# Routing tables and sums of a fused two-layer kernel in free columns of a PSUM bank

## The chip, the cores and the metric

The kernel runs on one core of one Trainium2 chip. A core has five engines that run their own instruction queues side by side: PE (TensorE, matrix products into PSUM), DVE (VectorE), ACT (ScalarE), POOL (GpSimd) and SP (SyncE, which starts transfers). SBUF is the working memory of all of them; PSUM, in eight banks of 2 KB a partition, is written by PE and read and written by VectorE and ScalarE. The metric is the device time of one execution in microseconds (us), as the median of several runs.

## What is computed

Four layers with residuals over x of 8 batches, 512 steps and 128 channels, all in float32: a bounded linear recurrence, one linear layer picked out of eight, a delta rule with 16 heads of 8 channels, and a mixture of 8 experts of which each token takes 2. The two that matter here, cut to the core:

```python
# the delta rule: S is 8 x 8 for each batch and head, 512 steps one after the other
def step(S, inp):
    q_t, k_t, v_t, beta_t = inp
    retrieval = jnp.einsum('bhij,bhj->bhi', S, k_t)
    S = S + jnp.einsum('bhi,bhj->bhij', beta_t * (v_t - retrieval), k_t)
    o_t = jnp.einsum('bhij,bhj->bhi', S, q_t)
    return (S, o_t)

# the experts: of 8, each token takes the 2 with the largest probability
logits = xf @ w_router
probs = jax.nn.softmax(logits, axis=-1)
topk_w, topk_idx = jax.lax.top_k(probs, TOP_K)
mask = jax.nn.one_hot(topk_idx, NUM_EXPERTS, dtype=xf.dtype)
weights = jnp.sum(topk_w[..., None] * mask, axis=1)
h = jax.nn.gelu(jnp.einsum('te,ieh->tih', xf, w1) + b1)
out = jnp.einsum('tih,ihe->tie', h, w2) + b2
out = jnp.sum(out * weights[..., None], axis=1)
```

## The kernel before

**Tiles and stages.** A tile is 128 tokens: 16 steps of 8 batches. The 32 tiles pass in nine pieces of 2, 4, 4, 4, 4, 4, 4, 4 and 2 tiles (SIZES) through the layers. For each piece `scanned`, `ssm_out` and `linear` do the first two layers, `delta_in` prepares keys, queries and the small triangular matrices of the delta rule (`tmat`, made by GpSimd), `delta_rule` runs the recurrence, `route` picks the experts. Pieces are gathered into groups (GROUPS) of one or two; when a group is complete, `experts` sorts its tokens by expert and runs them. The last piece has no sorting; `every_expert` runs all experts on it.

**The recurrence.** It goes in 128 blocks of 4 steps. Each block is six VectorE instructions, each of which needs the one before (lines 1404 to 1423): a sum of the 8 retrieval products of the block before (`st<-so`, 320 elements a partition), the product with the triangular matrix (`prod<-tmat,st`, 128), its sum (`st<-prod`), the product with the keys (`st<-kq,st`, 256), the sum onto the state (`st<-st`, 320) and the product of the state with keys and queries (`so<-kq,st`, 512). The state and all small sums of the recurrence live in two PSUM banks, `st0` and `st1`, in turn from block to block. Of their 512 columns, 320 hold the terms of the state (NS) and 32 the retrieval sums; the block's right-hand sides `u_16` take 128 more in `st1`. In `st0` the last 160 columns are not used. After each tile ScalarE copies `u_16` out (`upd<-st`).

**The routing.** `route` takes the two best experts of each token with VectorE's max and max_index (`best`, `besti`) and compares the indices with a table of 0 to 7, `iota8i`, to get one-hot masks (`mine`, once for each of the nine pieces). GpSimd then counts and weighs them. `experts` (five times, for the groups that are sorted) turns the counts into places: PE sums them over the tokens into a PSUM bank (`totals`, `earlier`), and VectorE makes from that, in thirteen small instructions and two more ahead of them (`mask`, `runf`): `full` (which blocks of 128 an expert fills, against a table `thresholds` of multiples of 128), `nblks`, `ends` and `starts` (blocks of each expert and their running sum), `place` (twice added to, then shifted by `starts`), `chosen` and `destf` (each token's two places), `dest` (the same as integers), `of_block` and `expert` (which expert a block belongs to, against a table `iotab` of 0 to 23), and `where` (twice: the rows at which that expert's weights start). GpSimd scatters the rows to `places` by `dest`; SP loads blocks of rows (`xb`) and an expert's first weights (`w1b`) by `where`; PE and ScalarE do the two layers (`ph`, `hid`, `po`), and GpSimd gathers the results (`back`).

**What sets the order.** A planner (`Plan`) records every operation and can lay them out by costs and due times. Here it does not: ORDER (line 383) lists all 4796 operations by number in a fixed order, and BANKS the PSUM bank of each product in turn; `ordered` (line 189) takes both as they are, so each engine's queue is this order. Routing instructions stand in VectorE's queue between those of the recurrence. What an instruction waits for is written by the framework below the planner, from what the instruction reads and writes; `region` and `depend` (lines 84 and 96) only serve the planner's own search for an order. A helper at line 330 issues nearly all operations, so most rows of the profile carry that line.

**Where the tables are.** `iota8i` and `iotab` are made at lines 866 to 883 with GpSimd's iota, `thresholds` at line 885 (tile at 884) by VectorE from `iotab`; `nblks`, `destf`, `expert` and `place` are tiles of SBUF (`gtile`). All of the routing's small instructions thus read SBUF alone, but for `runf` and the two sums of `place` (`totals` and `earlier` are in PSUM).

Of the kernel before, what the change touches and what calls it, by code (L numbers as in the profile page):

```python
# [16 lines left out]
P = 128  # L17
# [52 lines left out]
class Plan:  # L70
# [12 lines left out]
    @staticmethod  # L83
    def region(x):
        if isinstance(x, Bank):
            return x.owner, None, 0, 1, 0, 1
        name, dims, at = x.tensor.name, x.ap, x.offset
        if x.space == bass.MemoryType.DRAM:
            return name, None, 0, 1, at, at + sum((n - 1) * s for s, n in dims) + 1
        row = dims[0][0]  # L90
        p, f = divmod(at, row)
        if x.space == bass.MemoryType.PSUM:
            return name, None, 0, 1, 0, 1
        return name, None, p, p + dims[0][1], f, f + sum((n - 1) * s for s, n in dims[1:]) + 1
# [259 lines left out]
def _cost(engine, name, n, kw):  # L354
# [284 lines left out]
def seq_kernel(  # L639
# [215 lines left out]
    for base_, step in ((0, 1), (DH - 1, -1)):  # L855
# [7 lines left out]
            channel_multiplier=step,  # L863
        )

    iota8i = ctile([P, NE], "iota8i", U32)
    nc.gpsimd.iota(iota8i, pattern=[[1, NE]], base=0, channel_multiplier=0)

    before_ones = ctile([P, P], "before_ones")
# [24 lines left out]

    st = [bank(f"st{i}") for i in range(2)]
    NS = DH * B * (BL + 1)

    def terms(n):  # L900
# [1120 lines left out]
```

## Time and profile before

| what | us |
|---|---|
| median of 3 runs | 665.15 |
| lowest and highest of them | 662.67, 671.21 |
| the profiled execution's own time | 665.96 |
| its span, first to last instruction | 664.3 |
| PE busy | 526.6 (79%) |
| VectorE busy, 1290 instructions | 465.0 (70%) |
| ScalarE busy | 468.5 (71%) |
| GpSimd busy, 603 instructions | 458.8 (69%) |
| mean granted clock of PE | 0.915 |
| bytes moved by DMA | 110.16 MB, 166 GB/s |

The page divides the span into 40 slices of 16.6 us and gives each engine's busy share in tenths. Its chain of work that ended last follows back from the last instruction, at each step to what released it or to the instruction before it on its engine: VectorE holds 34% of the span, PE 26%, ScalarE 15%, GpSimd 12%. A group's row names line, engine, operation and tiles (written <- read), the shape and the count, then busy time, mean duration, and the idle time before it with what ended it. A row in order of time has the start, the duration, the engine and the same names. A duration counts from an instruction's start to its end, so what it waits for after its start is in it.

### The profile page before, as it was taken

The page shows a single profiled execution, that of the slowest core. Times are in us where ns is not written, and L with a number is a line of the kernel's source. Part 1 is how long each engine was busy: PE and PEld are TensorE (multiplying, and loading weights), DVE is VectorE, ACT ScalarE, POOL GpSimd, SP SyncE. Part 2 cuts the span into 40 slices and gives each one's busy share as a digit, 9 for nine tenths or more (in the row PEclk, how much of TensorE's full clock was granted, in tenths as well). Part 3 has the DMA queues.
Part 4 walks back from the last instruction along what each step waited for, and adds up shares of the span by engine and source line. Part 5 has one row for each costly group of instructions (what it writes and reads, how often), then busy time and mean ns, then how long its engine had stood idle before and what let it go on. Part 6 is the DMA issues. An engine that isn't in the chain of part 4 may idle for free.

```text
span 664.3 us, 10937 instructions
## 1 busy us (share of the span) xinstructions
PE 526.6 (79%) x3077; PEld 409.9 (62%) x3077; DVE 465.0 (70%) x1290; ACT 468.5 (71%) x984; POOL 458.8 (69%) x603
## 2 busy tenths in 40 slices
PE   3885668687796688796888787989969888879876
PEld 3653234454554465674676575787958887768775
DVE  6667158999988999989899998998991770002021
ACT  2875887879768579988899997857855654636421
POOL 6545567768768748899986978885588678454340
PEclk9899778989679789989899898999989999898988
DMA  4948145235243557446875576788877876766631
GB/s 127 318 136 273 56 117 144 64 84 154 64 127 74 160 144 189 132 128 171 213 193 152 145 193 176 208 233 224 220 227 199 236 226 216 203 207 191 169 103 35
DMA packets 96722, 110.16 MB, mean 166 GB/s; under 512 B 10180, under 2 KB 68207, under 8 KB 96663
## 3 DMA queue, kind: packets, MB, share of 16 engines
q1 hardware_dynamic: 91984, 101.31, 54.6%
q0 software_dynamic: 3904, 8.00, 4.3%
q8 instruction: 26, 0.43, 0.3%
q14 instruction: 34, 0.27, 0.1%
q10 hardware_dynamic: 774, 0.15, 0.1%
HBM read 85.90 MB, written 27.48 MB: 171 GB/s over the span
## 4 chain that ended last, share of the span: by engine, by line
DVE 34%; PE 26%; ACT 15%; POOL 12%; issue 6%; DMA 3%; another core or an unknown queue 2%; ACTq 1%; SPq 1%; DVEq 0%; POOLq 0%
DVE st L330 16%; PE in L330 9%; PE ph L330 8%; DVE so L330 6%; POOL places L1685 4%; PE po L1747 4%; ACT f L330 3%; PE po L330 3%; DVE prod L330 3%; ACT hid L330 2%; ACT L299 2%; ACT b L330 2%; POOL so L330 2%; PE in L1747 2%
## 5 line engine op out<-in xcount | busy, mean ns | idle before, releaser
L330 PE MATMUL ph<-xbT,w1b 128*128 128x128 f32 x760 | 141.1, 287 | 12.3 <-ACT xbT L330 5.5
L330 PEld LDWEIGHTS ph<-xbT,w1b 128*128 128x128 f32 x760 | 113.9, 199 | 19.6 <-ACT xbT L330 7.7
L330 ACT ACTIVATE hid<-ph 128x512 f32<-128x512 f32 x111 | 65.5, 598 | 78.4 <-PE ph L330 44.7
L1747 PE MATMUL po<-w_sb,hid 128*128 x536 | 104.4, 286 | 4.8 <-ACT hid L330 2.9
L1747 PEld LDWEIGHTS po<-w_sb,hid 128*128 128x128 f32 x536 | 84.0, 199 | 15.0 <-issue 9.4
L330 DVE TENSOR_TENSOR so<-kq,st 128x512 f32<-128x512 f32 x128 | 87.6, 684 | 5.6 <-PE in L330 0.6
L299 ACT ACT_TABLE_LOAD x64 | 82.1, 1283 | 8.9 <-DMA hid<-in_L_attn_ln_b_dram 7.8
L1685 POOL DMA_INDIRECT places<-xne,small_dest x60 | 60.0, 1000 | 19.6 <-issue 10.6
L330 POOL DMA_INDIRECT back<-results,small_dest x60 | 58.7, 978 | 21.1 <-issue 14.0
L330 DVE TENSOR_REDUCE st<-st 128x64 f32<-128x320 f32 x128 | 63.6, 497 | 3.7
L330 DVE TENSOR_REDUCE st<-so 128x32 f32<-128x320 f32 x128 | 62.8, 491 | 3.9 <-ACT so L330 0.8
L330 DVE TENSOR_TENSOR st<-kq,st 128x256 f32<-128x256 f32 x128 | 54.5, 426 | 3.5
L330 PEld LDWEIGHTS po<-wo,so 128*128 128x128 f32 x240 | 40.2, 213 | 23.4 <-POOL so L330 9.1
L330 PE MATMUL po<-wo,so 128*128 128x128 f32 x240 | 48.1, 303 | 8.3 <-POOL so L330 6.1
L330 PE MATMUL in<-b,wqkvb 128*128 128x512 f32 (+1 forms) x72 | 39.2, 635 | 11.5 <-ACT b L330 3.6
L1747 PE MATMUL in<-w_sb,hid 128*128 x224 | 45.6, 288 | 1.4 <-DVE small_where L330 1.0
L330 PE MATMUL in<-f,wT 128*128 128x512 f32 (+1 forms) x72 | 39.8, 646 | 8.3 <-DVE small_best L330 3.7
L330 DVE TENSOR_REDUCE st<-prod 128x32 f32<-128x128 f32 x128 | 37.2, 291 | 6.2 <-ACT upd L330 1.6
L330 DVE TENSOR_TENSOR prod<-tmat,st 128x128 f32<-128x128 f32 x128 | 36.3, 284 | 7.4 <-POOL tmat L330 4.2
L330 POOL TENSOR_TENSOR f<-f,f 128x512 f32<-128x512 f32 (+1 forms) x27 | 32.4, 1199 | 12.4 <-ACT f L330 12.3
L330 POOL TENSOR_TENSOR so<-so 128x512 f32<-128x512 f32 x24 | 31.3, 1304 | 11.4 <-DVE so L330 8.5
L330 POOL TENSOR_TENSOR fin<-fin,back 128x512 f32<-128x512 f32 (+1 forms) x14 | 16.8, 1198 | 29.9 <-ACT back L330 29.7
(339 smaller groups left out, 1380.3 us busy)
## 6 DMA issues: line engine op xcount, KB each, us to landing
kq<-scratch SPq DMA_DIRECT2D x64, 512.0 KB
w1b<-w1b_dram SPq DMA_DIRECT2D x103, 256.0 KB
xb<-places SPq DMA_DIRECT2D x20, 256.0 KB
results<-yb SPq DMA_DIRECT2D x20, 256.0 KB
places<-yb SPq DMA_DIRECT2D x2, 1472.0 KB
kq<-in_L_ffn_w_dram SPq DMA_DIRECT2D x2, 1024.0 KB
w1b_dram<-kq SPq DMA_DIRECT2D x2, 1024.0 KB
u_rows<-in_L_attn_u_dram SPq DMA_DIRECT2D x7, 256.0 KB
```

Source lines behind the costliest of these rows:

```text
L299: self.hw.scalar.preload_act_table_set(switch)
L330: return method(*(on(x) for x in args), **{k: on(x) for k, x in kw.items()})
L1685: rows_out = hw.gpsimd.indirect_dma_start(out=table[0 : nblk * P, :], out_offset=bass.IndirectOffsetOnAxis(ap=at, axis=0), in_=src, in_off ...
L1747: return hw.tensor.matmul(out_.on(nc.banks), lhsT=src, rhs=w2_f[:, bass.ds(at + c * P, P)], start=(c == 0), stop=(c == NHB - 1),)
```

## The change

Four of the routing's small sums and the two tables they are compared with move from SBUF to the 160 unused columns of `st0`: `iotab` (24 columns), `thresholds` (8), `nblks` (8), the last value of `place` (64), `destf` (16) and `expert` (23), 143 in all. `iota8i` and its iota on GpSimd are dropped: `mine` compares with the first eight columns of `iotab` instead, a float32 operand beside the uint32 indices. The first of the two sums of `place` stays in SBUF, the second writes PSUM. The clearing of `st0` at the start leaves the last 160 columns out. `region` keeps the columns of `st0` and `st1` apart for the planner. ORDER is the same with the number of the dropped iota taken out and those after it lowered by one; BANKS is unchanged.

```diff
-        if x.space == bass.MemoryType.PSUM:
+        if x.space == bass.MemoryType.PSUM and not name.startswith("st"):
             return name, None, 0, 1, 0, 1
...
-    iota8i = ctile([P, NE], "iota8i", U32)
-    nc.gpsimd.iota(iota8i, pattern=[[1, NE]], base=0, channel_multiplier=0)
...
-    iotab = ctile([P, MAXB + 1], "iotab")
+    st = [bank(f"st{i}") for i in range(2)]
+    NS = DH * B * (BL + 1)
+    spare = st[0][:, NS + B * BL :]
+    taken_of_spare = [0]
+
+    def spared(*shape):
+        n = math.prod(shape)
+        at = taken_of_spare[0]
+        taken_of_spare[0] = at + n
+        assert at + n <= N - NS - B * BL
+        return view(spare[:, at : at + n], [P, *shape])
+
+    iotab = spared(MAXB + 1)
     nc.vector.tensor_copy(iotab, iotabi)
-    thresholds = ctile([P, MAXT], "thresholds")
+    thresholds = spared(MAXT)
+    nblks_of, place_of, destf_of, expert_of = spared(NE), spared(NE * MAXT), spared(2, MAXT), spared(MAXB)
     nc.vector.tensor_scalar_mul(thresholds, iotab[:, 0:MAXT], float(P))
...
-    nc.vector.memset(st[0], 0.0)
+    nc.vector.memset(st[0][:, 0 : NS + B * BL], 0.0)
     nc.vector.memset(st[1], 0.0)
...
         nc.vector.tensor_tensor(
             mine,
-            iota8i.unsqueeze(1).unsqueeze(1).to_broadcast([P, 2, NT, NE]),
+            iotab[:, 0:NE].unsqueeze(1).unsqueeze(1).to_broadcast([P, 2, NT, NE]),
...
-        nblks = gtile([P, NE], "nblks")
+        nblks = nblks_of
...
-        nc.vector.tensor_add(place, place, earlier)
+        nc.vector.tensor_add(place_of[:, 0 : NE * nt], place, earlier)
+        place = place_of[:, 0 : NE * nt]
...
-        destf = gtile([P, 2, MAXT], "destf")[:, :, 0:nt]
+        destf = destf_of[:, :, 0:nt]
...
-        expert = gtile([1, MAXB], "expert")[:, 0:nblk]
+        expert = expert_of[0:1, 0:nblk]
```

More of the change, by code (lines that the diff above doesn't have):

```diff
@@ L893, in seq_kernel @@
     nc.vector.tensor_copy(iotap, iotapi)
-    st = [bank(f"st{i}") for i in range(2)]
-    NS = DH * B * (BL + 1)
     def terms(n):
```

490 rows, old and new, of the table ORDER are left out of this document.

## Prediction

> **What bounds the kernel now.** I read the page's engine rows and slices first, then the groups of VectorE by form, then single instructions in order of time, then the chain of waits. The slices say where VectorE can matter: it is 80 to 100% busy from the seventh slice (100 us) to the thirtieth (498 us), and idle for long stretches after that, where PE works through the experts.
>
> ```profile
> PE   3885668687796688796888787989969888879876
> DVE  6667158999988999989899998998991770002021
> POOL 6545567768768748899986978885588678454340
> ```
>
> The groups of VectorE show what the change is about: the same size of instruction takes two kinds of time.
>
> ```profile
> L330 DVE TENSOR_REDUCE st<-st 128x64 f32<-128x320 f32 x128 | 63.6, 497 | 3.7
> L330 DVE TENSOR_REDUCE st<-so 128x32 f32<-128x320 f32 x128 | 62.8, 491 | 3.9 <-ACT so L330 0.8
> L330 DVE TENSOR_TENSOR prod<-tmat,st 128x128 f32<-128x128 f32 x128 | 36.3, 284 | 7.4 <-POOL tmat L330 4.2
> L330 DVE TENSOR_TENSOR x<-po,base 128x128 f32<-128x128 f32 x15 | 4.3, 285 | 29.3 <-remote 20.0 <-PE po L330 9.3
> L330 DVE TENSOR_TENSOR small_mine<-iota8i,small_besti 128x64 f32<-128x64 uint32 x7 | 3.9, 564 | 0.0
> L330 DVE TENSOR_TENSOR small_starts<-small_ends,small_nblks 128x8 f32<-128x8 f32 x5 | 3.1, 614 | 0.0
> L330 DVE TENSOR_TENSOR small_chosen<-small_chosen,small_place 128x128 f32<-128x128 f32 x3 | 2.8, 930 | 0.0
> ```
>
> Products with one operand in PSUM (prod from st, x from po) average 284 and 285 ns for 128 elements, and in the per-tile view they never leave 256 to 295 ns in 143 executions, whatever GpSimd did. With both operands in SBUF, 8 elements (small_starts) average 614 ns and 128 (small_chosen) 930. The order of time shows why.
>
> ```profile
> 216.14 2.35 POOL L330 TENSOR_TENSOR both<-both,f 128x1024 f32<-128x1024 f32 x1
> 216.53 1.99 DVE L330 TENSOR_TENSOR small_starts<-small_ends,small_nblks 128x8 f32<-128x8 f32 x1
> 218.44 0.68 DVE L330 TENSOR_TENSOR so<-kq,st 128x512 f32<-128x512 f32 x1
> ```
>
> The instruction of 8 elements ends some 25 ns after the GpSimd instruction it ran into. The chain of waits has it in full:
>
> ```profile
> 215.68 0.53 DVE small_ends L330
> 216.22 0.10 DVE st L330
> 216.31 0.22 issue
> 216.53 1.99 DVE small_starts L330
> 218.51 0.60 DVE so L330
> ```
>
> **What is gained.** I went through each instruction the change touches and took its time less that of an unblocked one. Where a GpSimd instruction stood in front: mine 991, 1544 and 541 against 216 (2.43 us); starts 1985 and 620 against 159 (2.29); ends 623 and 608 against 160, and one of 221 (0.97); chosen 520, 1056 and 1215 against 285 (1.94); full 666, 479 and 290 against 165, 175 and 216 (0.88); place 731 against 203 (0.53); of_block 682 against 329 (0.35); where 1245 and five of 208 to 361 against 155 (1.7). Sum 11.1 us of VectorE. The thresholds at 2.5 us took 2081 ns against 152 for a small one out of PSUM (logs from ph), 1.9 us more.
>
> Only what the chain holds moves the end. At 212 to 219 us it runs through full, ends and starts: 0.50 + 0.46 + 1.83 = 2.8. At 229 us it goes through the GpSimd sum of so that mine (991 ns) stands behind, so prod comes 0.7 earlier. At 274 to 282 it holds of_block, starts, chosen and one where: 0.35 + 0.46 + 0.24 + 0.2 = 1.25. At 392.6 it waits 0.85 us behind chosen: 0.77. Sum 5.5 us. Off the chain lie the mine of 1544 ns at 332.8 (the chain is on GpSimd from 327 to 336.5), that at 371.6 (ScalarE and PE), ends and place at 388 to 390 (ScalarE), chosen at 474.3 (ScalarE's table load, 474.0 to 475.3) and full and where after 541 (PE, ScalarE). The thresholds and the removed iota (125 ns of GpSimd at 8.4 us) are covered by the loads that the chain waits for until 11.1 us: nothing. mask, a copy within SBUF that also waited (657 ns), stays.
>
> **What is paid.** Nine mine and thirteen instructions in each of five routings, 74, get an operand or result in PSUM; 54 read PSUM where they read SBUF alone. From rows: a reduce of 320 elements takes 497 ns out of PSUM and 491 out of SBUF, so 54 x 6 ns = 0.3 us. Results: st from prod, 295 ns, against destf, 268, both reducing 128 elements: 27 ns for 20 results, 0.5 us. A third of both is on the chain, 0.3. [...]
>
> The larger price is a wait. The tables share the bank st0 with the recurrence's state, and this trace shows waits kept by bank, not by columns:
>
> ```profile
> 484.85 0.29 DVE L330 TENSOR_REDUCE st<-prod 128x32 f32<-128x128 f32 x1
> 485.18 0.43 DVE L330 TENSOR_TENSOR st<-kq,st 128x256 f32<-128x256 f32 x1
> 485.64 0.50 DVE L330 TENSOR_REDUCE st<-st 128x64 f32<-128x320 f32 x1
> 486.17 0.27 ACT L330 COPY upd<-st 128x128 f32<-128x128 f32 x1 [4.13 <-DVE st L330]
> ```
>
> ScalarE's upd copies columns that st from prod finished at 485.14, yet it starts 30 ns after the reduce that merely uses the same bank. Only VectorE touches st0, so no other engine gets a wait, but on VectorE neighbours now overlap and would stop doing so:
>
> ```profile
> 387.84 0.21 DVE L330 TENSOR_TENSOR small_place<-small_runf,in 128x64 f32<-128x64 f32 x1
> 387.97 0.21 DVE L330 TENSOR_REDUCE small_nblks<-small_full 128x8 f32<-128x64 f32 x1
> 388.10 0.21 DVE L330 TENSOR_TENSOR small_place<-small_place,in 128x64 f32<-128x64 f32 x1
> ```
>
> They start 0.13 apart and last 0.21. Counting in VectorE's order every pair of neighbours that overlaps, has one of the 74 in it, and would have one of the two writing st0, I find 44, each losing 0.05 to 0.11 us: 4.4 us. On the stretches of the chain named above (and 472 to 478) that is 2.7 us. Whether an engine gets such waits on itself the trace can't show: bounds 0 and 2.7 on the chain. I take 2.7, as the copies on ScalarE are kept by bank every time. Behind a waiting routing instruction stands the recurrence's next, and behind that the sums of so on GpSimd and PE; this is why I count the wait in full.
>
> Net on the chain: 5.5 - 0.3 - 2.7 = 2.5 us. The profiled execution took 665.96 (span 664.3 plus 1.7 around it), so 663.5; it lay 0.8 above the median of 665.15, so **662.6 us** in the median. Late next are the scatters on GpSimd (283 to 334 us) and PE with its weight loads after 500; GpSimd is 70% busy from 236 to 270, so it can start earlier.
>
> **Rivals.**
> - Hidden by what follows. From 283 to 334 us the chain is GpSimd's, after 490 PE's and the DMAs'. Against it: the scatters wait for dest, which VectorE writes. Time: 665 less half a us, 664.5.
> - Slower: the waits by bank cost more than the lock. It happens where a routing instruction and the recurrence around it line up so that none overlaps. If GpSimd's stretch swallows what is gained before it, 4.4 of waits and 0.8 of PSUM on top of the median less the 0.77 and 0.7 kept gives 668.9. It decides from 5.2 us on the chain. At most, two lost overlaps of 0.1 us for each of 74 are 14.8 us: 680. [...]
> - All of it gained: the off-chain waits were about to be the chain. 11.1 us: 654.1. With the thresholds' 1.9 and the 2.5 us by which GpSimd's slowed instructions (those over 120 ns above the shortest of their form) exceed that shortest, 15.5: 649.7.
> - The change doesn't do it: an instruction with one SBUF operand still waits. Against: 143 executions at 256 to 295 ns. Time 665 to 668.
>
> **How the numbers follow.** Chances: the forecast 0.47, its own range 659.9 (no waits by bank) to 665; hidden 0.15; slower 0.18, half of it over 2%; all gained 0.15, two thirds over 2%; no effect 0.05. Two per cent, 13.3 us, is about what a measurement of this kernel can tell from no change; its runs lie 8.5 us apart (662.67 to 671.21). So faster by over 2% 0.10, slower 0.09, within 0.81. The range goes from 654.1 less the 2.5 us of the lowest run, 652, to 668.9 plus half of the highest run's 6.1, 672; 0.19 is left out.
>
> **What would show it.** In the changed profile mine, starts and ends lie near 216, 160 and 175 ns at most; the chain at 212 to 219 us is 2.8 us shorter. If the waits by bank are there, neighbours like those at 387.8 start 0.23 apart instead of 0.13. The recurrence's last product, at 544.3 us now, comes 2 to 6 us earlier. It is wrong if small instructions with a table in PSUM still last as long as GpSimd's beside them, if the recurrence ends later than now, or if it ends earlier and the span doesn't follow.

## The result and the profile after

| what | before | after |
|---|---|---|
| median of 22 runs each, us | 667.1 | 663.06 |
| lowest and highest, us | 662.67, 671.21 | 658.68, 665.26 |
| the profiled execution's span, us | 664.3 | 661.3 |
| VectorE busy in it, us | 465.0 | 458.0 |
| mean granted clock of PE | 0.915 | 0.909 |

The ratio of the times is 0.9938, 95% interval 0.992 to 0.9956: faster by 4.1 us (2.9 to 5.3), well below the 2% that count as a difference. The change was measured twice more, as x8 and x10 below, 0.9952 (0.9915 to 0.9989) and 0.993 (0.9897 to 0.9962); weighted by their intervals the three give 0.9939 (0.9924 to 0.9953). Every ratio in this document is taken from the fast runs alone and is not the ratio of the two medians beside it, which lies up to 0.003 away (x3: 0.9975 for a ratio of 0.9945; x8: 0.9974 for 0.9952).

VectorE's busy tenths in the page of the changed kernel, 40 slices of 16.5 us:

```profile
DVE  7667158999988999889799998998991760002021
```

The shape is that of before: a VectorE near its limit from 100 to 490 us. Some groups of VectorE's instructions, forms apart (busy us, mean ns of one | idle before):

```profile
L330 DVE TENSOR_TENSOR prod<-tmat,st 128x128 f32<-128x128 f32 x128 | 36.4, 285 | 7.4 <-POOL tmat L330 4.2
L330 DVE TENSOR_TENSOR small_mine<-st,small_besti 128x64 f32<-128x64 f32 x7 | 1.6, 222 | 0.1
L330 DVE TENSOR_TENSOR small_chosen<-small_chosen,st 128x128 f32<-128x128 f32 x3 | 0.9, 289 | 0.3
L330 DVE TENSOR_TENSOR small_starts<-small_ends,st 128x8 f32<-128x8 f32 x5 | 0.8, 154 | 0.0
L330 DVE COPY small_mask<-follows 128x32 f32<-128x32 f32 x1 | 0.7, 668 | 0.0
```

The recurrence's own `prod` costs what it did (285 ns, 284 before). mine fell from a mean of 564 ns to 222, starts from 614 to 154, chosen from 930 to 289: the waits that stood in these durations are gone. Added up over the trace, the 74 instructions that the change touches took 26.2 us before and 15.6 after. mask, which the change leaves in SBUF, still takes 668 ns. The chain of waits at the place where starts had held it for 1.99 us (start, us, what):

```profile
215.60 0.17 DVE small_ends L330
215.77 0.10 DVE st L330
215.87 0.21 issue
216.08 0.15 DVE small_starts L330
216.24 0.66 DVE so L330
```

From the end of `ends` to `so` the chain now spends 0.47 us, of which `starts` has 0.15. The new waits are there as well: at the place that answers to 387.8 us of before,

```profile
386.63 0.21 DVE L330 TENSOR_TENSOR small_place<-small_runf,in 128x64 f32<-128x64 f32 x1
386.76 0.22 DVE L330 TENSOR_REDUCE st<-small_full 128x8 f32<-128x64 f32 x1
387.01 0.23 DVE L330 TENSOR_TENSOR st<-small_place,in 128x64 f32<-128x64 f32 x1
387.28 0.17 DVE L330 TENSOR_TENSOR_SCAN small_ends<-ones,st 128x8 f32<-128x8 f32 x1
```

the first two, of which only one writes `st0`, still start 0.13 us apart; the next two pairs, where both use it, 0.25 and 0.27.

**The ledger by blocks.** One block of the recurrence goes from one `so` product to the next. The length of most blocks hardly depends on how early the block starts (the one at 206.38 us is 2.90 us long, and 2.90 again where it starts at 206.55 in the first profile of the changed kernel and at 203.25 in x8), so two traces can be compared block by block. Of the blocks whose length changed, those at the moved instructions came out as follows (start and length before; difference in the changed kernel, in the first profile and in the two of the later runs x8 and x10):

```
 start  length  after     x8    x10   routing instructions in it
177.55   3.13   +0.10  +0.10  +0.11   mine
209.28   4.00   -0.37  -0.81  -0.45   runf, mask, full
213.28   5.16   -2.03  -2.03  -2.03   place, place, nblks, ends, starts
218.44   2.99   +0.35  +0.35  +0.36   of_block, place, chosen, destf, dest, expert, where
228.28   3.78   -0.58  -0.58  -0.58   mine
270.21   2.96   +1.25  +0.26  +0.26   full, place, place
273.17   4.31   -0.29  -0.29  -0.29   nblks, ends, of_block, starts, place, chosen, destf
277.48   4.03   +0.06  +0.07  +0.07   dest, expert, where
284.71   3.04   -0.15  -0.15  -0.15   where
332.20   4.22   -1.32  -1.33  -1.33   mine
336.42   3.11   +0.29  +0.30  +0.29   (the block behind it)
370.47   3.22   -0.19  -0.20  -0.20   mine
386.53   4.66   -0.58  -0.57  -0.57   full, place, nblks, place, ends, starts, place
391.18   4.43   -0.05  -0.05  -0.05   of_block, chosen, destf, dest, expert, where
469.65   3.48   +0.40  +0.39  +0.41   full, place, nblks, place, ends, starts
473.13   4.30   -0.11  -0.11  -0.10   place, chosen, destf, dest, of_block, expert
534.14   3.49   +0.12  +0.12  +0.12   mine
```

But for the block at 209 us, where mask itself took 0.22 us in x8, and one cell at 270, they agree within 0.02 us. With 0.37 shorter at 209 and 0.26 longer at 270 they sum to 4.1 us shorter. Two blocks with moved instructions are left out, as they differ from execution to execution: the one at 465.9 us, with another mine (+0.18, +0.12, -0.25), and the last, at 537.6, with the fifth routing (-0.16, -0.39, -1.57). Blocks without routing are left out as well, and not all of them are neutral. In the one at 318 us VectorE waits for PE's product `po`, 1.31 us before and 2.07, 1.52 and 2.25 in the three profiles of the changed kernel, and the block became 0.76, 0.21 and 0.94 us longer. So the 4.1 us are a gain in the blocks of routing, not yet one at the end.

### The profile page after: what moved, and what is told of

Its sections match the earlier page's. It is cut to its first block, busy times and chain, and to the rows that moved or that the text cites. A ratio compares the mean times of both kernels' runs of the same rounds, so it can differ in the third digit from the quotient of the medians.

```text
span 661.3 us, 10932 instructions
## 1 busy us (share of the span) xinstructions
PE 527.5 (80%) x3077; PEld 410.6 (62%) x3077; DVE 458.0 (69%) x1290; ACT 469.1 (71%) x984; POOL 458.5 (69%) x602
## 4 chain that ended last, share of the span: by engine, by line
DVE 33%; PE 30%; ACT 15%; POOL 10%; issue 6%; DMA 3%; another core or an unknown queue 2%; SPq 1%; ACTq 1%; DVEq 0%; POOLq 0%
DVE st L330 16%; PE in L330 11%; PE ph L330 9%; DVE so L330 6%; PE po L330 4%; POOL places L1695 4%; PE po L1757 4%; ACT f L330 4%; ACT L299 3%; DVE prod L330 3%; ACT hid L330 2%; PE in L1757 2%; ACT b L330 2%; POOL f L330 1%
## 5 line engine op out<-in xcount | busy, mean ns | idle before, releaser
L1757 PE MATMUL po<-w_sb,hid 128*128 x536 | 105.8, 289 | 3.1 <-issue 2.4
L1757 PEld LDWEIGHTS in<-w_sb,hid 128*128 128x128 f32 x224 | 34.7, 195 | 5.6 <-issue 5.0
```

What stands on the lines that cost most here:

```text
L1757: return hw.tensor.matmul(out_.on(nc.banks), lhsT=src, rhs=w2_f[:, bass.ds(at + c * P, P)], start=(c == 0), stop=(c == NHB - 1),)
```

## The experiments

The first four stand against the kernel before on one chip (its median there 665.89 in 29 runs).

**x1: the waits without the tables.** The kernel before; VectorE's instructions that would share `st0` wait for each other as if they did, all tables and sums stay in SBUF.

```diff
+                if op.st0:
+                    table, reads, writes = op.st0
+                    behind = last.get((not table, True)) if not writes else max(
+                        (last[k] for k in ((not table, True), (not table, False)) if k in last), default=None
+                    )
+                    if behind:
+                        wait = mybir.DependencyInfo(mybir.DependencyClass.Sync, mybir.DependencyReason.DATA)
+                        self.tc.add_manual_dep(made.ins, behind[1], wait, reason="as if in one bank")
```

> The kernel before, its tables in SBUF, with the waits alone that the shared bank brings: each routing instruction waits for the recurrence's neighbour that would touch st0, and the other way round. Theory (the waits by bank are the price of the change): 1.0 to 2.7 us slower than the kernel before, ratio 1.0015 to 1.004, less than the 2.7 counted where a routing instruction stands behind GpSimd anyway; in the trace full, place and nblks start 0.23 to 0.25 us apart where they started 0.13 apart, and starts, mine and chosen still last 0.5 to 2 us. Rival (a wait on the engine's own predecessor costs nothing): ratio 1.000 with its interval on both sides of it.

Measured: 668.73 us, ratio 1.0033 (1.0002 to 1.0064), 2.2 us slower (0.1 to 4.3). Seven blocks with routing in them are longer by 0.14 to 1.02 us, 2.6 in all; left out are the one at 270, where VectorE stood idle for PE, the one at 332, where mine took 0.76 us beside one GpSimd instruction instead of 1.54 beside two and the block was 0.79 shorter, and three with a mine that are 0.1 to 0.2 us longer. So the waits cost time here: in the block at 273, `nblks`, the sum of `so` and `ends` start 0.25 and 0.53 us apart in x1, as in the changed kernel, where they started 0.13 and 0.39 apart before. Their size in time is known only to lie between 0.1 and 4.3 us, and not all of the 2.6 us is spacing: in that block `ends`, started later, took 0.52 us instead of 0.22, up to the end of a GpSimd instruction. The spacing of full, place and nblks that was expected is not there (0.13 us as before): x1's waits are only those between routing and recurrence, and between two routing instructions, such as 386.76 and 387.01 above, it adds none.

**x2 and x3: the halves of the change.** x2 moves the table that mine compares with, nothing else. x3 moves everything else and leaves mine with its table in SBUF.

```diff
+    iota8 = st[0][:, NS + B * BL : NS + B * BL + NE]
+    nc.vector.tensor_copy(iota8, iotabi[:, 0:NE])
...
-            iota8i.unsqueeze(1).unsqueeze(1).to_broadcast([P, 2, NT, NE]),
+            iota8.unsqueeze(1).unsqueeze(1).to_broadcast([P, 2, NT, NE]),
```

> Only the nine mine read a table in PSUM (0 to 7, in st0); all tables and sums of the sorting stay in SBUF. Theory (what counts is the waiting on the chain): the mine of 991 ns was on the chain, those of 1544 and 541 ns were not, so 0.7 us faster than before, ratio 0.999, at most 0.997. Rival (every wait of VectorE counts): 2.4 us of 11, ratio 0.9964, and more than a third of the change's 4.1 us. In the trace all nine mine under 230 ns, starts, ends and chosen as long as before.

> The change without mine: thresholds, iotab and the four sums in st0, mine compares with iota8i in SBUF as before. Theory: the chain at 212 to 219 us and at 274 to 282 us held 2.8 and 1.25 us of these and 0.77 at 392, so most of the change's 4.1 us is here: 2.5 to 3.7 us faster than before, ratio 0.9945 to 0.9962. Rival (every wait counts): the same 2.5 or so that are left after mine's, ratio 0.9975 to 0.996. In the trace three mine of 0.3 to 1.3 us beyond 216 ns, all of the sorting's instructions short.

Measured: x2 666.59 us, ratio 0.9994 (0.9966 to 1.0023); x3 664.25 us, 0.9945 (0.9912 to 0.9978). In x2 all nine mine are short:

```profile
L330 DVE TENSOR_TENSOR small_mine<-st,small_besti x9: 190/211/225, 180.3 to 604.7; 128x64 f32<-128x64 f32 x7, 128x32 f32<-128x32 f32 x2
```

and the blocks of mine change as in the whole change (-0.58 at 228, -1.34 and then +0.30 at 332, -0.21 at 370). The other blocks with routing keep their length within 0.02 us, but for the one at 386, longer by 0.33. What x2 leaves in SBUF need not take the same time twice: mask, which the changed kernel leaves there too, took 0.67 us in its first profile and 0.22 in x8. Which instruction it is at 386 was not shown. In x3 the blocks of the sums change as in the whole change (-2.03 at 213, -0.29 at 273, -0.58 at 386), and those of mine at 228 and 370 do not (0.00 and -0.01). By the ratios most of the time comes from the sums, though the two intervals overlap between 0.9966 and 0.9978. Whether mine adds to it, the interval of x2 (2.3 us faster to 1.5 slower) leaves open. In x2's trace the recurrence's last product comes at 544.5 us, no earlier than before: blocks without mine (0.49 us longer at 318, 0.41 at 382, 0.73 at 528, with waits for PE and for a transfer) took back what those with mine had gained.

**x4: the same step backwards.** The kernel before with the recurrence's retrieval sums `w`, one operand of each `prod`, taken out of PSUM; its other operand, `tmat`, is in SBUF. The sum that writes `w` from `so` then reads and writes SBUF alone as well.

```diff
+    sums = [ctile([P, B * BL], f"w{i}") for i in range(2)]
...
-        return st[n % 2][:, NS : NS + B * BL].rearrange("p (b t) -> p b t", t=BL)
+        return sums[n % 2].rearrange("p (b t) -> p b t", t=BL)
```

> The kernel before with one thing moved the other way: the recurrence's retrieval sums w lie in SBUF and not in st0 and st1, so that each of the 128 products prod reads both operands from SBUF. Theory (two SBUF operands stand behind a GpSimd instruction that is under way): the 39 instructions of that kind in the routing waited 9.4 us, 0.24 each; 128 of them on the recurrence's chain are 31 us at that rate, and what slack the recurrence has takes some: 10 to 31 us slower, ratio 1.015 to 1.047, with prod from 284 ns at the mean to 400 and more and single ones over 1 us. Rival (PSUM isn't what frees them; the routing's instructions were slow for their small size or their place): prod stays within 256 to 300 ns, ratio 1.000.

Measured: 706.97 us, ratio 1.062 (1.0554 to 1.0687), 41 us slower. The rows of the tile `w`, shortest, middle and longest duration in ns:

```profile
L330 DVE TENSOR_REDUCE w<-so x128: 457/485/489, 90.5 to 584.2; 128x32 f32<-128x320 f32 x128
L330 DVE TENSOR_TENSOR prod<-tmat,w x128: 260/293/5698, 94.3 to 585.3; 128x128 f32<-128x128 f32 x128
```

Half of the 128 products are as fast as ever and the mean goes from 284 to 655 ns, so 47.6 us more of VectorE: with its second operand in SBUF the same form took anything from 260 to 5698 ns. The longest, 5.70 us from 458.21, ends 0.16 us after a row of GpSimd instructions without a gap that runs from 457.67 to 463.75; that GpSimd's work of the moment sets the length is read from ends like this one. The sums `w<-so`, with one operand and the result in SBUF, stayed within 457 to 489 ns in 128 executions. So reading and writing SBUF alone did not make every instruction wait; `prod`, with a second operand there, waited. The price was above the range expected.

The next three, x5 to x7, ask whether what the change left can be had, and what becomes of its gain at 270 us (the kernel before on this chip: 667.71, 17 runs). In the first profile of the changed kernel VectorE stood idle there until PE's sums were done:

```profile
270.41 0.29 DVE L330 TENSOR_TENSOR_SCAN small_runf<-follows,in 128x64 f32<-128x64 f32 x1 [0.85 <-PE in L330]
```

**x5: base and mask on ScalarE.**

```diff
-        normalised(x2, rstd, shift, tiles_of(base), 0, g == 0)
+        normalised(x2, rstd, shift, tiles_of(base), 0)
...
-            nc.vector.tensor_copy(mask.rearrange("p (e i) -> p e i", e=NE), follows[:, :, 0:nt])
+            (nc.scalar.copy if nt == 4 else nc.vector.tensor_copy)(mask.rearrange("p (e i) -> p e i", e=NE), follows[:, :, 0:nt])
```

> The changed kernel, with two instructions that still read SBUF alone and still last long beside GpSimd moved to ScalarE: base of the first piece (two of 1.29 us at 60.5 us, 2.51 together) and the mask of the second group (0.67 us at 211.1 us). Theory (what a table in PSUM cannot reach still waits for GpSimd, and the wait counts where VectorE holds the chain): base ends near 61.6 instead of 63.06, the scan z starts 0.9 earlier (GpSimd's decay then sets it), and the recurrence comes 0.3 to 0.5 us earlier still behind 211. If it is carried to the end, 0.8 to 1.4 us off the changed kernel: ratio to the kernel before 0.992 (0.990 to 0.994). Rival (the first 95 us end on loads and PE, and what is gained at 211 is given back behind 270): as the changed kernel, 0.9938; in the trace z earlier, but the recurrence's first product not.

**x6: two instructions exchanged** in ORDER: 2466 (ScalarE's `f`) behind 2172 (its copy out of the bank), 1687 (`earlier`) right behind 1686 (`totals`).

> The changed kernel with two instructions of the order exchanged around 268 us: ScalarE's f_7<-f_7 (0.72 us) goes behind its copy f<-in, which empties the bank that the totals' product needs, and PE's earlier stands right behind totals. Theory (the 0.85 us for which VectorE's runf stands idle at 270.4 us in the changed kernel is the gain handed back to ScalarE and PE, by that bank): the idle time is gone (under 0.2 us), and the recurrence lies some 2 us ahead of the kernel before at 282 us, where the changed kernel lay 1.28 ahead; by the end 0 to 0.8 us of it is left, as at 322 us the chain is on PE and ScalarE: ratio 0.9925 to 0.994. Rival (the hand-over at 270 is not set by that bank but by GpSimd's b and so beside it): idle 0.6 to 0.9 as now, recurrence 1.3 ahead, ratio 0.9938.

**x7: both.**

> Both edits together on the changed kernel. Theory: their gains add up to 270 us (recurrence 2.5 to 3.5 us ahead of the kernel before at 282), and 1 to 2 us of the sum is left at the end: ratio 0.991 (0.989 to 0.9935). Rival (GpSimd, PE and ScalarE between 283 and 334 us take it all back): 0.9938, as the changed kernel.

Measured: 659.16, 660.21 and 661.38 us; ratios 0.9876 (0.9835 to 0.9917), 0.989 (0.9848 to 0.9933) and 0.9886 (0.9856 to 0.9916). In x5 the recurrence's first `so` comes at 99.3 us, 98.6 in the first profile of the changed kernel: nothing is gained at the start, as the rival had it. In x6 the idle time at 270 is gone and the block there is 0.26 longer than before instead of 1.25; but in x5, where nothing was exchanged, it is 0.26 as well. That three kernels with different edits all lie some 0.005 below the first ratio of the changed kernel made the chip a suspect, so the changed kernel was run beside them.

**x8 and x9: the changed kernel and x7 on one chip** (kernel before: 666.12, 17 runs).

> The changed kernel once more, unaltered, so that it and the next run share a chip and the runs of the kernel before. Theory (the change gives 3 to 5 us, by what it measured): ratio 0.992 to 0.9956. In its trace the recurrence lies 2.2 to 2.6 us ahead of the kernel before at 232 to 267 us, as in its first profile; whether VectorE stands idle 0.85 us at 270 us again shows if that hand-over belongs to the order (it comes again) or to one execution (it does not). Rival: the first ratio was one chip's, here 0.996 or more.

> The kernel with both edits once more (base and mask on ScalarE, the two instructions exchanged at 268 us), beside the changed kernel on the same chip. Theory (waits behind GpSimd that the change left, and the hand-over at 270 us, are on the path to the end): 2 to 4 us below the changed kernel, ratio to the kernel before 0.986 to 0.991. Rival (what the edits gain ahead of 540 us is lost after it, where PE and its weight loads set the end, as in the profiled execution of the first run): as the changed kernel, 0.992 to 0.996.

Measured: x8 664.36 us, ratio 0.9952 (0.9915 to 0.9989); x9 660.3 us, 0.9908 (0.9875 to 0.9942). x8 settles the hand-over: unaltered, the changed kernel has no idle time there in this execution, its block is +0.26, and from 209 to 232 us the recurrence gains 3.1 us on the kernel before, 2.66 in the first profile and the rest from mask. The 0.85 us at 270 are in one of the three profiles of the changed kernel. In x8 the recurrence lay 6.2 us ahead at 232 us, not the 2.2 to 2.6 expected, for another reason, told below. x9, 4.1 us below x8 in the median, came out as its theory had it; the next three do not repeat it.

**x10 to x12: the changed kernel, x5 and x7 on one chip** (kernel before: 648.99, 29 runs).

> The changed kernel once more, as the measure for the next two on the same chip. Theory (a gain of some 4 us, by the blocks of the recurrence that hold a moved instruction, which come out alike to 0.05 us in three executions: 4.1 us shorter in all): ratio 0.991 to 0.996. Rival (the ratios of the changed kernel differ by chip as much as by kernel): outside of that.

> The changed kernel with base of the first piece and the mask of the second group on ScalarE. Theory (what is shown of it in the recurrence is one block at 209 us, shorter by 0.82 instead of 0.38 us): 0.4 us below the changed kernel, which is not to be told from it: ratios within 0.002. Rival (the start of the program is on the path to the end, and 0.9 to 1.9 us are gained there as well): 1.5 to 3 us below, a ratio lower by 0.002 to 0.0045.

> That, and the two instructions exchanged at 268 us. Theory (the hand-over at 270 us was one execution's): as the run before, within 0.002. Rival (it recurs in most executions): 0.5 to 1 us lower than the run before.

Measured: 642.95, 644.31 and 644.52 us; ratios 0.993 (0.9897 to 0.9962), 0.9946 (0.9916 to 0.9975) and 0.9925 (0.9895 to 0.9955). Neither edit is to be told from the changed kernel. Moving mask is seen in its block (0.82 shorter instead of 0.45 at 209 us) and nowhere in the time; no version here is shown to beat the changed kernel. The idle time at 270 us is not in x10 either.

## Why the prediction was right, and where it was not

**The gain.** Right in kind: the durations of mine, starts, ends and chosen fell to those of their forms, and x4 shows the reverse with a loss ten times the gain. By place, what was said to be gained on the chain against what the blocks show, the new waits included: 209 to 221 us, 2.8 against 2.05; 229, 0.7 against 0.58; 270 to 285, 1.25 against 0.11; 386 to 395, 0.77 against 0.62. Where the old wait was one long instruction (starts, 1.99 us), nearly all of it came through; where it was three or four short ones, the new waits ate it. In the kernel before, the block at 273:

```profile
273.77 0.21 DVE L330 TENSOR_REDUCE small_nblks<-small_full 128x8 f32<-128x64 f32 x1
273.90 0.48 DVE L330 TENSOR_REDUCE st<-so 128x32 f32<-128x320 f32 x1
274.29 0.22 DVE L330 TENSOR_TENSOR_SCAN small_ends<-ones,small_nblks 128x8 f32<-128x8 f32 x1
...
275.24 0.62 DVE L330 TENSOR_TENSOR small_starts<-small_ends,small_nblks 128x8 f32<-128x8 f32 x1
275.79 0.27 DVE L330 TENSOR_REDUCE st<-prod 128x32 f32<-128x128 f32 x1
```

and in x8, the changed kernel again:

```profile
267.91 0.23 DVE L330 TENSOR_REDUCE st<-small_full 128x8 f32<-128x64 f32 x1
268.18 0.49 DVE L330 TENSOR_REDUCE st<-so 128x32 f32<-128x320 f32 x1
268.70 0.17 DVE L330 TENSOR_TENSOR_SCAN small_ends<-ones,st 128x8 f32<-128x8 f32 x1
...
269.24 0.14 DVE L330 TENSOR_TENSOR small_starts<-small_ends,st 128x8 f32<-128x8 f32 x1
269.31 0.27 DVE L330 TENSOR_REDUCE st<-prod 128x32 f32<-128x128 f32 x1
```

From `ends` to the sum of `prod` 1.50 us became 0.61, as forecast; but `nblks`, the sum of `so` and `ends`, which had started 0.13 and 0.39 us apart, now start 0.27 and 0.52 apart, and the block ahead of it and the one behind lose 0.26 and 0.07 in the same way.

**The price.** Right in kind and somewhat high. That VectorE gets waits on itself by bank, which the trace of before could not show, is shown by the spacing above: the instructions at 386.76, 387.01 and 387.28 each use other columns of `st0` than the one ahead, and start 0.25 and 0.27 us apart where it was 0.13 before. x1 writes such waits between routing and recurrence, with the same spacing (0.25), and puts their price between 0.1 and 4.3 us. On the four places 5.5 us of gain left 3.36, so 2.1 were paid if the 5.5 came in full; with the 0.29 net at 469 to 478 it is 2.4, where 2.7 of waits and 0.3 of PSUM were taken. In the changed kernel they are seen alone where no old wait was: +0.35, +0.26 and +0.40 in the blocks at 218, 270 and 469. The cost of an operand in PSUM is as small as taken: `nblks` went from 0.21 to 0.23 us at 273, `st` from `small_chosen`, which was destf, from 0.27 to 0.29.

**The step that failed.** "Off the chain lie the mine of 1544 ns at 332.8 (the chain is on GpSimd from 327 to 336.5), that at 371.6 (ScalarE and PE)". The block at 332 became 1.33 us shorter and only 0.30 came back in the next, in each of the profiles of this kernel, and 0.2 at 370 stayed. In the kernel before mine outlasted there two GpSimd instructions that follow each other without a gap:

```profile
332.69 0.91 POOL L330 TENSOR_TENSOR qkp<-qkp,upd 128x384 f32<-128x384 f32 x1
332.79 1.54 DVE L330 TENSOR_TENSOR small_mine<-iota8i,small_besti 128x64 f32<-128x64 uint32 x1
333.56 0.66 POOL L330 TENSOR_TENSOR b<-b,dots 128x128 f32<-128x128 f32 x1
```

In the changed kernel it takes 0.22. The chain ran over GpSimd in that stretch of that one execution; the recurrence stood behind mine all the same. The same holds in part for the chosen at 474.3 that the prediction put behind ScalarE: without its wait the `prod` behind it starts 1.79 us after `so` instead of 2.27, and most of that is lost again in the block, which x1's waits alone made 0.37 us longer. So the ledger is: 3.36 on the four places, 1.23 for these two mine, less 0.29 at 469 to 478 and 0.22 in two blocks of mine that became longer, 4.1 us. The net forecast was 2.5. That 4.1 is also what was measured agrees, but the time has an uncertainty of 1 us, and x2 does not resolve mine alone; that its 1.2 us reach the end is not shown: in x2's trace they were gone before the recurrence ended.

**The number.** 662.6 was forecast and 663.06 measured, closer than the steps deserve, by luck: the kernel before came out at 667.1 in the 22 runs beside it, not 665.15, so 1.6 us of gain too little met a start 1.95 too low.

**The rivals.** No effect falls by the durations. Hidden by what follows would have left half a us, and the interval of the gain begins at 2.9; x1, a loss on the recurrence alone, points the same way, though its interval begins at 0.1. Part of it happens all the same, as the waits for PE at 318 us show. Slower by the waits was right in kind and not in size: 2.2 us, not 5.2. What it calls the lock is the time that instructions stood beside GpSimd, 1.99 us for starts; the runs show the durations and no lock. All of it gained, 11.1 us, nearly came true for VectorE, 10.7 us less in the instructions touched, and not for the kernel, 4.1. The new waits make up some 2.4 of the difference by the estimate above; that the rest lay off the chain fits the forecast, but no run tests it one instruction at a time. Of the signs named in the prediction, the short durations and the wider spacing were there. The stretch from 209 to 221 us became 2.05 us shorter, new waits included, and not the 2.8 named. The last product of the recurrence moved from 544.3 us to 542.8 in the first profile, less than the 2 us named at least, and to 538.3 and 536.2 in x8 and x10, which says more of the executions than of the change.

## What to carry to other kernels

An instruction of VectorE with two operands in SBUF can stretch beside GpSimd: `starts` took 0.15 to 1.99 us in the kernel before, `prod` in x4 0.26 to 5.70. Look for it as one form whose longest execution is a multiple of its shortest, and give it one operand in PSUM; mine went from 1.54 us at most to 0.23. Free columns of a bank that the same engine is busy in are not free here: neighbours that came to share `st0` lost their overlap, though their columns differ, and started 0.25 to 0.27 us apart instead of 0.13, 0.12 to 0.14 us a pair. So move the instructions with one long wait, and count the pairs around those with short ones. To judge a few us in a kernel whose executions differ by more, compare the lengths of a recurring block as well as the times, and do not take a shorter block for a shorter kernel.

## What the runs showed of the hardware

**Which instructions waited beside GpSimd.** In the kernel before, several with two SBUF operands did (starts up to 1.99 us against 0.15, chosen 1.22 against 0.29), and so did some with a single one: the copy mask (0.66 us), base (1.30 each) and one `where` (1.25 against 0.15). The sums over one SBUF operand did not: `nblks`, `destf` and `expert` stay between 158 and 325 ns there, and `w<-so` in x4 between 457 and 489. Of the sums that were moved, these three were never slow themselves; `starts`, `ends` and `where`, which read two of them, were.

**PE's clock and the block at 181 us.** Two blocks without moved instructions, at 181 and 199 us, were 1.52 and 1.00 us shorter in x8 than before and within 0.1 us of it in the first profile. Activity from 175 to 185 us (PE, its weight loads, VectorE, ScalarE, GpSimd, then PE's granted clock), first profile of the changed kernel:

```profile
175.00:185.00 10.00, 8.12 (x29) 4.98 (x28) 8.43 (x28) 6.73 (x18) 5.36 (x12) 0.67 0.29 68
```

and x8:

```profile
175.00:185.00 10.00, 8.01 (x29) 4.14 (x27) 9.69 (x30) 7.69 (x21) 4.87 (x9) 0.90 0.19 45
```

In the first profile, at 0.67, VectorE waited 1.33 us for PE at the end of this stretch (1.42 in the kernel before, at 0.67 as well); in x8, at 0.90, it did not: the same kernel. The two products `in<-f,wT` that it waits for took 2.08 us in the one and 1.13 in the other. In x10 the clock is 0.66 there, and the block at 181 is as long as before. It is as short as in x8 in x5, x9 and x12 too, with clocks of 0.82 to 0.86, and in no other run, where the clock is 0.66 or 0.67. The block at 199 does not go with this stretch: in x10 it is 1.01 us shorter although the clock was 0.66. VectorE waits there 1.1 us for ScalarE's `upd` before and in the first profile, and not in x8 and x10; why is left open.

**The last 120 us are another matter.** From the recurrence's last product to the end it was 119.9 us in the profile of before, 118.5, 120.1 and 103.5 in the three of the changed kernel, 126.1 in x7. On the chip of x10 PE did more in the same time, at a higher clock and a higher rate of transfers: from 580 to 600 us it was busy for 18.33 us with 151 products at a clock of 1.00 and 236 GB/s, in x8 for 16.04 us with 109 at 0.83 and 182 GB/s. In x8 the chain holds five waits of 2.3 to 5.7 us after 560 us that the profile puts down to another core or an unknown queue, 18.9 us in all; the first profile has four such, 11.5 us, and x10 none. What differs between these chips, or beside them, no run here tells.
